# A four-layer graph network on one core: factors of a dense column moved between engines, and layer 2's block ends put in another order

## The chip, the cores and the metric

The kernel runs on one NeuronCore of a Trainium2 chip. The core has a matrix engine (TensorE, PE in the profile, with its weight loads shown apart as PEld), a vector engine (VectorE, DVE), a scalar engine (ScalarE, ACT), a general engine (GpSimd, POOL) and a queue engine (SyncE, SP). Each works through its own instructions in the order in which the program lists them, and waits at an instruction until what it needs is there; what stands behind it waits too. Sixteen DMA engines move data between the chip's main memory (HBM) and the on-chip memory (SBUF). Matmul results arrive in PSUM[...].

The metric is device microseconds (us) of one execution. The median of the runs shown decides.

## The reference

Four layers work on one graph of 3327 nodes with 512 features each. Every layer's result is added to its input and normalised over the features: `x = layernorm(x + layer(x, adj))`.

- Layer 0: graph attention, 8 heads of 64. Layer 1: mean over all neighbours, two dense maps. Layer 2: mean over the first 64 neighbours, two dense maps with a leaky ReLU.
- Layer 3: graph attention with 4 heads of 128, whose weight is built from quaternion parts. This is the layer that the change touches most:

```python
h = jnp.einsum('nf,hfo->hno', x, hamilton)
f_src = jnp.einsum('hno,ho->hn', h, a_src)
f_dst = jnp.einsum('hno,ho->hn', h, a_dst)
e = jax.nn.leaky_relu(f_src[:, :, None] + f_dst[:, None, :], ALPHA)
e = jnp.where((adj > 0)[None, :, :], e, NEG_INF)
attn = jax.nn.softmax(e, axis=-1)
h_prime = jnp.einsum('hnm,hmo->hno', attn, h)
```

with ALPHA = 0.2. The graph is uneven: an edge is the likelier the lower the two node numbers. So the first 128 nodes have many neighbours, and most nodes have some of those first 128 among theirs.

## The kernel before

**Blocks.** The nodes are cut into 26 blocks of 128 rows (NB = 26; the last has 127). Block 0 is nearly dense in both directions and is treated apart: its row (block 0 as the receiver, `row0`) and its column (block 0 as the source for every other block, `col0`) are dense 128 x 128 masks. All other edges are kept as lists. For block b a list has up to `NEAR[b]` places (1920 for block 1, down to 512 for the last three), in chunks of 128: 15 chunks for block 1, 4 for blocks 23 to 25.

**A group** is up to four chunks of one block. For each chunk GpSimd issues an indirect DMA that gathers 128 table rows from HBM (L1018, `gather`) into a ring of buffers. In layer 3 a group then passes these steps (`Gat.group`): distances `far` and the 0/1 matrix `ds` (ScalarE L1308, VectorE L1318), scores of the receivers by small matmuls (L1332), `sc` and its maximum (VectorE L1345, L1347), exponentials (ScalarE L1348, L1349), the selection matrix `sel` (L1353), the gathered rows times their weights (VectorE L1356), and matmuls into the block's sums in PSUM (L1375). Between the steps the generator yields.

**The order of the work** is written out by generators. `work` holds those of the groups, `ends` those of the block ends; `both()` lets every live generator of `work` take one step and then every one of `ends` (oldest first; in layer 3 newest first). One call of `both()` is a program step. In layer 2 and 3 the program order of each engine is just the order in which these steps issue instructions, and the tile framework adds the waits.

**Layer 2's ends and layer 3's projection** (`layer2_end`). When a block's neighbour sums are complete (matmuls L1879, with L1871 for block 0's column), its end divides (L2071), adds, takes the norm (L2073 to L851), and writes the new row block into `xres[b]`. Then it becomes the input of layer 3: `transposed` turns it by four TensorE transposes (L789) into PSUM and ScalarE copies the four parts to `xt` (L796), adding up row sums; `products` multiplies with the weights `w3` into two PSUM halves of two heads each (L1056, 16 matmuls, tile `po`, two buffers); `write` copies each half to the table rows `tg` (L1067, one buffer) and the scores `fall` (L1068), and stores the rows to HBM. `first_block` takes, from the same halves, the exponentials `ul` (L1241) and a copy of the features `G` (L1242), then a mask (L1244); on VectorE it makes the weights of this block as a source for block 0 (L1249, L1251). The matmuls with them, L1263, are issued by `catch_up`, one block at a time while groups are running; later blocks are put aside and done in `finish`.

Three things hold a block back in `layer2_end`: block 0 must have been opened (`opened`: `open_first` finds the bound `nmost` that all `ul` use), a space for G must be free (two spares of its own, and room in the ring once the last gather has been listed), and `g3.free` must be set. The block that passes clears `free`; `first_block` sets it after the mask.

After the last block's `write`, `head` finds the maxima over all nodes and stores three special table rows, on which layer 3's first gather waits. `finish` then computes, among others, `sh`, turns it by TensorE and stores it to the HBM scratch `e_d` (L1128), rows in the order head, block.

**Block 0's column in layer 3.** For every block b, `column` loads the exponentials of its 128 receivers for the four heads, the same to all 128 partitions (L1407, tile `upc`, three buffers), waits four steps, and makes the factors: four ScalarE instructions, `relu(rcol * up - 1)`, one per head because the scale is a value per partition and head (L1412); one step later one VectorE instruction adds 1 and applies the mask `col0` (L1414). The block's last group issues eight matmuls with them (L1372) ahead of its last chunk's. `open_column` prepares the other side once: it loads block 0's table rows to `gcol` (L1388), and from their scores makes `rcol` and the weights by which the rows are scaled (L1395 to L1400).

**Layer 3's ends** (`layer3_end`, `summed`): divide (L1522, L1523, L1526), ELU and residual (L1536, L1538, L1540), norm (L1541, L1542, L1552, L1553, L1556 to L1558), scale (L855), store.

Of the kernel before, what the change touches and what calls it, by code (L numbers as in the profile page):

```python
# [8 lines left out]
F32 = mybir.dt.float32  # L9
# [9 lines left out]
ALU = mybir.AluOpType  # L19
# [612 lines left out]
def sparse_path(ctx, tc, flag_i, x, adj, l0_w, l0_a1, l0_a2, l1_w_self, l1_b_self, l1_w_nb, l1_b_nb,  # L632
# [406 lines left out]
    class Gat:  # L1039
        def __init__(self, name, table, H, OUT, w, k):  # L1040
# [5 lines left out]
            self.opened, self.free = False, True  # L1046
# [12 lines left out]
        def write(self, b, pool, pw):  # L1059
# [5 lines left out]
            for s in range(2):  # L1065
# [3 lines left out]
                               by_head[:, :, 0:OUT + 2:OUT + 1].rearrange("p h k -> p k h"))  # L1069
            store(self.table, b, tb.rearrange("p h m -> p (h m)"), 2)  # L1070
# [37 lines left out]
        def finish(self, pool, ps):  # L1108
# [9 lines left out]
            if self.k:  # L1118
# [9 lines left out]
                nc.sync.dma_start(e_d, es)  # L1128
# [104 lines left out]
        def first_block(self, b, pool, pw, G, wt):  # L1233

            H, OUT = self.H, self.OUT
            hh = H // 2
            m = LAST if b == NB - 1 else P
            ul = pool.tile([P, H, 2], F32, name="ul")
            for s in range(2):
                by_head = pw[s].rearrange("p (h m) -> p h m", h=hh)  # L1240
                nc.scalar.activation(ul[:, s * hh:(s + 1) * hh, :], by_head[:, :, OUT + 1:], AF.Exp, bias=self.nmost)  # L1241
                nc.scalar.copy(G[:, s * hh:(s + 1) * hh, :OUT], by_head[:, :, 1:OUT + 1])  # L1242
            mask = pool.tile([P, P], F32, name="mk", bufs=1)
# [137 lines left out]
        def open_column(self, pool):  # L1381
# [6 lines left out]
            nc.sync.dma_start(gcol, self.table[2:2 + P, :])  # L1388
            self.gcol = gcol.rearrange("p (h m) -> p h m", m=M)
            self.rcol = pool.tile([P, H], F32, name="rcol", bufs=1)  # L1390
            self.low = pool.tile([P, 1], F32, name="low", bufs=1)
            nc.vector.memset(self.low, -1.0)
# [3 lines left out]
            nc.scalar.activation(self.rcol, low, AF.Exp, scale=1.0 - GAT_ALPHA)  # L1396
            nc.scalar.activation(self.gcol[:, :, OUT], low, AF.Exp, scale=GAT_ALPHA)
# [5 lines left out]
        def column(self, b, pool):  # L1403
# [3 lines left out]
            nc.sync.dma_start(up, bass.AP(tensor=e_d.tensor, offset=e_d.offset + b * P,  # L1407
                                          ap=[[0, P], [NB * P, H], [1, P]]))
            for _ in range(4):
                yield  # L1410
            for h in range(H):
                nc.scalar.activation(up[:, h, :], up[:, h, :], AF.Relu, bias=self.low, scale=self.rcol[:, h:h + 1])  # L1412
            yield
            nc.vector.scalar_tensor_tensor(up, up, 1.0, col0[:, b, None, :].to_broadcast([P, H, P]),  # L1414
                                           ALU.add, ALU.mult)
# [611 lines left out]
    with ExitStack() as lay:  # L2027
# [38 lines left out]
        def layer2_end(b, acc):  # L2066
# [12 lines left out]
            while b and not (g3.opened and (g3.spare or g3.space) and g3.free):  # L2079
                yield  # L2080
# [135 lines left out]
```

## Time and profile before

| what | value |
|---|---|
| median of 3 runs | 1661.63 us (1660.79 to 1669.61) |
| the profiled execution | 1659.49 us |
| its span, first to last instruction | 1657.7 us |
| TensorE matmuls busy | 1487.2 us (90%) |
| VectorE busy | 1175.7 us (71%) |
| ScalarE busy | 903.4 us (54%) |
| GpSimd busy | 762.6 us (46%) |
| TensorE weight loads busy | 998.9 us (60%) |
| mean granted TensorE clock | 0.955 |
| layer 3's projections (L1056) | 1158.2 to 1391.6 us of the span |
| layer 3's gathers | 1397.65 to 1614.04 us of the span |

A line of the profile names the source line, the engine, the operation, and what it writes and reads by the program's tile names, with shapes as partitions x elements. In a timeline the first number is the start in us from the beginning of the span and the second the time taken; `x4` says that four such instructions were merged into one line, `[1.41 <-ACT xt L796]` that the engine sat idle for 1.41 us until that instruction released it. In a view of stretches each engine's busy time is followed by its number of instructions. A view of waits gives the total in us, how often, and the longest. Instructions of one engine overlap at their edges, so a sum of durations is above the time that they occupy.

### The profile page before, as it was taken

Reading aid. Unit: us, or ns where it says so; the run is one execution under the profiler, and the core shown is the slowest. Engines: PE = TensorE matmul, PEld = TensorE weight load, DVE = VectorE, ACT = ScalarE, POOL = GpSimd, SP = SyncE. Lnnn points to the kernel's source line nnn. Section 1 sums busy time; section 2 is a strip of 40 time slices with the busy share of each in tenths; the row PEclk is TensorE's granted clock in tenths of the full one; section 3 lists DMA queues with packets and bytes.
Section 4 is the critical chain, followed back from the end, with each engine's and each line's share of the span. In section 5 each row is a group of like instructions: output and inputs, shape, how many; then the busy total and the mean of one; then the engine's idle time right before and its main releaser. Section 6 shows DMA issues by size and latency. Waiting matters only on the chain.

```text
span 1657.7 us, 24457 instructions
## 1 busy us (share of the span) xinstructions
PE 1487.2 (90%) x7305; PEld 998.9 (60%) x7341; DVE 1175.7 (71%) x3136; ACT 903.4 (54%) x3007; POOL 762.6 (46%) x994
## 2 busy tenths in 40 slices
PE   6789968999999999889999999887999996988885
PEld 4567746666666777435555555433566665777764
DVE  7998789998567789215566677648665644779886
ACT  5788865777667878412222121212344444679997
POOL 3000057665554520055444565137777702777770
PEclk9889979999999999879999999999999999999998
DMA  8877678876665542199788999348899812888881
GB/s 253 267 240 263 194 254 280 269 214 207 204 192 152 169 140 81 52 367 317 246 298 312 326 371 337 132 143 296 297 322 295 285 52 91 241 240 249 255 248 64
DMA packets 130402, 381.99 MB, mean 230 GB/s; under 512 B 22037, under 2 KB 36477, under 8 KB 130259
## 3 DMA queue, kind: packets, MB, share of 16 engines
q0 software_dynamic: 67696, 252.97, 47.6%
q1 hardware_dynamic: 62563, 127.35, 22.8%
q8 instruction: 60, 0.98, 0.2%
q14 instruction: 83, 0.68, 0.1%
HBM read 331.89 MB, written 48.37 MB: 229 GB/s over the span
## 4 chain that ended last, share of the span: by engine, by line
PE 63%; DVE 11%; ACT 9%; DMA 8%; issue 5%; POOL 3%; SPq 0%; ACTq 0%; DVEq 0%; POOLq 0%
PE po L806 19%; PE acc L1375 12%; PE po L1056 10%; PE acc L1879 9%; PE pt L789 3%; DMA gl<-t_d,idx 3%; DMA gt<-t_d,idx 1%; PE acc L1871 1%; PE acc L1263 1%; DVE gt L1356 1%; PE acct L1485 1%; DVE cand L909 1%; ACT m L882 1%; ACT upc L1412 1%; POOL gl L1018 1%
## 5 line engine op out<-in xcount | busy, mean ns | idle before, releaser
L1018 POOL DMA_INDIRECT gt<-t_d,idx x201 | 203.8, 1014 | 342.3 <-DVE eq L978 208.0
L1018 POOL DMA_INDIRECT gl<-t_d,idx x265 | 269.6, 1017 | 134.8 <-DMA t_d<-t 51.4
L1375 PE MATMUL acc<-gt,sel 128*128 128x264 f32 (+3 forms) x804 | 209.9, 408 | 4.4 <-DVE gt L1356 2.7
L1018 POOL DMA_INDIRECT gm<-t_d,idx x140 | 140.4, 1003 | 143.9 <-PE acc L1879 95.6
L806 PE MATMUL po<-wn,xt 128*128 128x512 f32 x416 | 193.9, 608 | 7.1 <-ACT h L1526 3.8
L1375 PEld LDWEIGHTS acc<-gt,sel 128*128 128x128 f32 (+3 forms) x804 | 153.4, 200 | 42.0 <-issue 13.9
L1375 PE MATMUL acc<-gl,sel 128*128 128x260 f32 (+3 forms) x524 | 137.5, 410 | 11.0 <-ACT r L1553 4.9
L806 PEld LDWEIGHTS po<-wn,xt 128*128 128x128 f32 x416 | 77.8, 194 | 89.1 <-issue 76.2
L1056 PE MATMUL po<-gt,xt 128*128 128x268 f32 x416 | 118.1, 428 | 14.1 <-ACT g0fall L1068 8.2
L1356 DVE TENSOR_TENSOR gt<-gt,pg 128x1536 f32<-128x1536 f32 (+3 forms) x64 | 116.6, 1822 | 13.6 <-ACT sel L1351 13.3
L792 ACT COPY xt<-pt 128x512 f32<-128x512 f32 x81 | 47.3, 588 | 130.8 <-PE pt L789 117.6
L1879 PE MATMUL acc<-gm,selr 128*128 128x512 f32 (+3 forms) x324 | 110.9, 462 | 7.3 <-DMA gm<-t_d,idx 5.0
L1375 PEld LDWEIGHTS acc<-gl,sel 128*128 128x128 f32 (+3 forms) x524 | 100.4, 201 | 27.1 <-ACT r L1553 5.2
L909 DVE MAX8 cand<-val 128x8 f32<-128x464 uint16 (+32 forms) x184 | 107.6, 620 | 0.1
L1056 PE MATMUL po<-w,xt 128*128 128x262 f32 x416 | 97.0, 386 | 8.0 <-ACT xt L796 5.1
L1018 POOL DMA_INDIRECT gk<-t_d,idx x65 | 65.7, 1011 | 82.3 <-DMA t_d<-mean 60.0
L1056 PEld LDWEIGHTS po<-gt,xt 128*128 128x128 f32 x416 | 79.2, 203 | 32.8 <-ACT g0fall L1068 8.6
L1308 ACT ACTIVATE far<-place,sites 128x128 int16<-128x128 int16 (+3 forms) x167 | 87.3, 543 | 13.1 <-DVE ds L1318 12.1
L806 PE MATMUL po<-wx,xt 128*128 128x512 f32 x208 | 93.6, 595 | 0.3 <-ACT vc L967 0.3
L789 PE MATMUL pt<-s_ident,xres 128*128 128x128 f32 x500 | 77.5, 283 | 17.7 <-POOL gt L1668 10.5
L806 PE MATMUL po<-wl,xt 128*128 128x512 f32 x208 | 93.1, 593 | 0.0
L1056 PEld LDWEIGHTS po<-w,xt 128*128 128x128 f32 x416 | 78.2, 190 | 24.0 <-ACT xt L796 9.8
(397 smaller groups left out, 3222.4 us busy)
## 6 DMA issues: line engine op xcount, KB each, us to landing
ab<-in_adj_dram SPq DMA_DIRECT2D x25, 832.0 KB
ab<-in_adj_dram SPq DMA_DIRECT2D x25, 831.5 KB
t_d<-t SPq DMA_DIRECT2D x25, 512.0 KB
gm<-t_d POOLq DMA_DIRECT2D x21, 512.0 KB
t_d<-t SPq DMA_DIRECT2D x25, 384.0 KB
t_d<-tg SPq DMA_DIRECT2D x25, 264.0 KB
gd<-t_d SPq DMA_DIRECT2D x25, 264.0 KB
t_d<-tg SPq DMA_DIRECT2D x25, 260.0 KB
```

The costliest lines, as they stand in the source:

```text
L789: nc.tensor.transpose(pt[:, c, :], src[:, c * P:(c + 1) * P], ident)
L792: nc.scalar.copy(xt, pt)
L806: nc.tensor.matmul(po, xt[:, c, :], w[:, c], start=c == 0, stop=c == DC - 1)
L882: nc.scalar.activation(m[:, c0:], ab[s][:, c0:], AF.Sign, accum_out=half[:, s, b:b + 1])
L909: nc.vector.max(out=cand[:, s, :], in_=val[:, cuts[s]:cuts[s + 1]])
L1018: nc.gpsimd.indirect_dma_start(out=t[:m, c, :], out_offset=None, in_=table[:, :], in_offset=bass.IndirectOffsetOnAxis(ap=l.idx[:m, c0 + c: ...
L1056: nc.tensor.matmul(pw[s], xt[:, c, :], self.w[:, c, s, :], start=c == 0, stop=c == DC - 1)
L1263: nc.tensor.matmul(self.acc[h // hh][:, h % hh, :], wt[:m, h, :], G[:m, h, :], start=False, stop=False)
L1308: nc.scalar.activation(o, place[:, (c0 + q0) * P:(c0 + q1) * P], AF.Abs, bias=l.nmid[k], scale=2.0)
L1356: nc.vector.tensor_mul(Gc[:, :, :OUT], Gc[:, :, :OUT], w[:, :g].rearrange("p c (h o) -> p (c h) o", o=1).to_broadcast([P, g * H, OUT]))
L1375: nc.tensor.matmul(accs[b][s], S[:m, c, :], G[:m, c, s * hh * M:(s + 1) * hh * M], start=at + c == 0, stop=last)
L1879: nc.tensor.matmul(accs[b], chosen, parts[:, k * D:(k + 1) * D], start=at + c + k == 0, stop=k == top and at + c == n - 1)
```

## The change

In layer 3, `column` makes the factors by VectorE alone: four instructions per block, one per head, each of which takes the larger of the loaded value and a value per partition (`least`) and multiplies with the mask. To make that the same product, `open_column` scales block 0's rows with the exponential of the full difference and keeps the reciprocal ratio in `least`. The factors are made in the step in which ScalarE's part was before, so the block's entry in `factors` is there one step earlier. `e_d` is stored in the order block, head, so that a block's load is one contiguous run. In `open_column` the load of `gcol` is issued where it was, and everything that uses it comes two steps later; a memset is gone.

In layer 2's ends, a block is turned (transposes and copy to `xt`) before it waits for the gate, not after it. A counter, `holding`, lets one block be turned and waiting until block 0 is open, and two after that. What needs the halves for block 0's sums, `ul` and `G`, is made in `lift`, which `write` calls after each half; for block 0 itself, whose bound is not there yet, it is called after `open_first`.

```diff
-            self.opened, self.free = False, True
+            self.opened, self.free, self.holding = False, True, 0
...
-        def write(self, b, pool, pw):
+        def write(self, b, pool, pw, lift=None):
...
+                if lift is not None:
+                    lift(s)
             store(self.table, b, tb.rearrange("p h m -> p (h m)"), 2)
...
-                nc.sync.dma_start(e_d, es)
+                nc.sync.dma_start(bass.AP(tensor=e_d.tensor, offset=e_d.offset,
+                                          ap=[[P, H], [H * P, NB], [1, P]]), es)
...
-        def first_block(self, b, pool, pw, G, wt):
-
-            H, OUT = self.H, self.OUT
-            hh = H // 2
-            m = LAST if b == NB - 1 else P
-            ul = pool.tile([P, H, 2], F32, name="ul")
-            for s in range(2):
+        def lifted(self, ul, G, pw):
+
+            OUT, hh = self.OUT, self.H // 2
+
+            def lift(s):
                 by_head = pw[s].rearrange("p (h m) -> p h m", h=hh)
                 nc.scalar.activation(ul[:, s * hh:(s + 1) * hh, :], by_head[:, :, OUT + 1:], AF.Exp, bias=self.nmost)
                 nc.scalar.copy(G[:, s * hh:(s + 1) * hh, :OUT], by_head[:, :, 1:OUT + 1])
+
+            return lift
+
+        def first_block(self, b, pool, ul, G, wt):
+
+            H = self.H
+            m = LAST if b == NB - 1 else P
...
             nc.sync.dma_start(gcol, self.table[2:2 + P, :])
+            for _ in range(2):
+                yield
             self.gcol = gcol.rearrange("p (h m) -> p h m", m=M)
-            self.rcol = pool.tile([P, H], F32, name="rcol", bufs=1)
-            self.low = pool.tile([P, 1], F32, name="low", bufs=1)
-            nc.vector.memset(self.low, -1.0)
+            self.least = pool.tile([P, H], F32, name="least", bufs=1)
             yield
             low = pool.tile([P, H], F32, name="lowf", bufs=1)
             nc.vector.tensor_sub(low, self.gcol[:, :, OUT], self.cmax)
-            nc.scalar.activation(self.rcol, low, AF.Exp, scale=1.0 - GAT_ALPHA)
-            nc.scalar.activation(self.gcol[:, :, OUT], low, AF.Exp, scale=GAT_ALPHA)
+            nc.scalar.activation(self.least, low, AF.Exp, scale=GAT_ALPHA - 1.0)
+            nc.scalar.activation(self.gcol[:, :, OUT], low, AF.Exp)
...
-            nc.sync.dma_start(up, bass.AP(tensor=e_d.tensor, offset=e_d.offset + b * P,
-                                          ap=[[0, P], [NB * P, H], [1, P]]))
+            nc.sync.dma_start(up.rearrange("p h i -> p (h i)"),
+                              bass.AP(tensor=e_d.tensor, offset=e_d.offset + b * H * P, ap=[[0, P], [1, H * P]]))
             for _ in range(4):
                 yield
             for h in range(H):
-                nc.scalar.activation(up[:, h, :], up[:, h, :], AF.Relu, bias=self.low, scale=self.rcol[:, h:h + 1])
-            yield
-            nc.vector.scalar_tensor_tensor(up, up, 1.0, col0[:, b, None, :].to_broadcast([P, H, P]),
-                                           ALU.add, ALU.mult)
+                nc.vector.scalar_tensor_tensor(up[:, h, :], up[:, h, :], self.least[:, h:h + 1], col0[:, b, :],
+                                               ALU.max, ALU.mult)
...
+            while b and g3.holding > g3.opened:
+                yield
+            g3.holding += 1
+            xt = transposed(fin, ps, xres[b], g3.xsum, b)
+            yield
             while b and not (g3.opened and (g3.spare or g3.space) and g3.free):
                 yield
+            g3.holding -= 1
             g3.free = False
             G, wt = g3.spaces()
-            xt = transposed(fin, ps, xres[b], g3.xsum, b)
-            yield
             pw = g3.products(ps, xt)
             yield
-            g3.write(b, fin, pw)
+            ul = fin.tile([P, H3, 2], F32, name="ul")
+            lift = g3.lifted(ul, G, pw)
+            g3.write(b, fin, pw, lift if b else None)
             if b == 0:
                 yield from g3.open_first(fin, ps, pacc0)
+                for s in range(2):
+                    lift(s)
             if b == NB - 1:
                 g3.head(fin, ps)
-            yield from g3.first_block(b, fin, pw, G, wt)
+            yield from g3.first_block(b, fin, ul, G, wt)
```

## The prediction

> **What bounds the kernel now.** I read the busy time of each engine in stretches first, because the page's 90% for TensorE averages over four layers. The cuts are where layer 2's projections begin (1180.4), where its last neighbour matmul ends (1368.4), where its last projection ends (1391.6), and two places in layer 3.
>
> ```profile
> core 0: us, PE busy (x) PEld busy (x) DVE busy (x) ACT busy (x) POOL busy (x), PEclk, DMA share, GB/s
> 1180.40:1368.40 188.00, 185.13 (x945) 128.74 (x963) 110.08 (x280) 83.12 (x419) 108.74 (x110) 1.00 0.73 246
> 1368.40:1391.60 23.20, 17.06 (x80) 13.66 (x79) 10.00 (x28) 11.48 (x64) 0.00 (x0) 1.00 0.10 39
> ...
> 1542.80:1628.60 85.80, 74.20 (x477) 59.58 (x474) 76.31 (x224) 81.77 (x258) 54.96 (x54) 0.92 0.79 230
> 1628.60:1657.70 29.10, 12.32 (x59) 10.08 (x57) 13.61 (x47) 18.32 (x49) 0.00 (x0) 0.74 0.14 49
> ```
>
> Layer 2 is TensorE's: idle 2.9 of 188 us, then 6.1 of 23.2. Layer 3's second half is ScalarE's (81.8 of 85.8 us), with VectorE close (76.3). Next the timeline, TensorE alone, at layer 2's end:
>
> ```profile
> 1369.43 3.80 PE L1056 MATMUL po<-w,xt 128*128 128x262 f32 x16 [0.46 <-ACT xt L796]
> 1373.07 0.60 PE L789 MATMUL pt<-s_ident,xres 128*128 128x128 f32 x4
> 1375.08 3.80 PE L1056 MATMUL po<-w,xt 128*128 128x262 f32 x16 [1.41 <-ACT xt L796]
> ...
> 1387.82 3.77 PE L1056 MATMUL po<-w,xt 128*128 128x262 f32 x16 [2.85 <-DVE xt L800]
> ```
>
> A projection each 5.65 us, 3.64 of it matmuls; the rest waits for xt, which ScalarE copies only after it has emptied the block before. Four projections come after the last neighbour matmul.
>
> Then layer 3's gathers and scores. These lines of GpSimd's and VectorE's timelines belong together:
>
> ```profile
> 1613.09 0.95 POOL L1018 DMA_INDIRECT gk<-t_d,idx  x1 [0.30 <-issue]
> ...
> 1628.59 0.20 DVE L1345 TENSOR_TENSOR sc<-pg,gk 128x32 f32<-128x32 f32 x1
> ```
>
> The last gather is issued by 1614.04; the score that needs it comes 14.6 us later. Going through all 57 groups so, the lag is 3 to 5 us up to 1543 (where the score itself waits 0.79 us for a gather) and then grows. GpSimd issues one gather each 1.25 us (0.95 busy, 0.30 between) from 1397.65 on, 165 of them, and is never held long. So up to about 1543 the gathers set the pace; after it the engines that work on them do, and fall some 10 us behind. Last, who VectorE and ScalarE wait for, from 1542.8 to 1628.6 and in the groups of layer 3:
>
> ```profile
> DVE upc L1414 <- ACT upc L1412: 3.4, 9, 0.6
> DVE h L1538 <- ACT e L1536: 2.9, 7, 0.6
> ...
> L1412 ACT ACTIVATE upc<-upc,low,rcol 128x128 f32<-128x128 f32 x100 | 40.8, 478 | 0.0
> L1414 DVE SCALAR_TENSOR_TENSOR upc<-upc,col 128x512 f32<-128x512 f32 x25 | 17.3, 691 | 6.2 <-ACT upc L1412 6.0
> ```
>
> **What the Trainium skill says.** "Perfetto Trace Analysis", section Identifying the Most-Contended Engine: for Vector and Scalar, occupancy names the bottleneck; the stretch above agrees with it (95% ScalarE). Section Optimizing Scalar/DVE Operations there: each instruction carries an overhead, so that larger ones pay if the engine is saturated; the change cuts one instruction into four. "VectorE: DVE Perf Modes", the section on the TRN2 errata: a fixed latency per instruction, paid per tile. The trace agrees: SCALAR_TENSOR_TENSOR takes 160 ns on 128x1 and 691 on 128x512. "ScalarE: Activation LUTs", Rules for kernel authors: relu, max and mul belong on VectorE; here 478 ns on ScalarE against 342 for a two-operation TENSOR_SCALAR of that shape (L1249).
>
> **Part 1, the factors.** Removed from ScalarE: four L1412 per block, 1.63 us end to end; 25 blocks, 40.8 us. On VectorE one L1414 goes, after which the next instruction starts 0.61 us later (1631.69 to 1632.30), and four SCALAR_TENSOR_TENSOR of 128x128 come. No row has them. From below: 160 ns at one element and 691 at 512 make about 293 at 128; less the 0.08 by which L1414 overlaps its successor, 0.21 each, 0.84 for four. From above: L1249's four take 1.11 us, 0.258 apart, so 1.03. I take 0.95: plus 0.34 per block. In 1542.8 to 1628.6 lie 11 blocks: VectorE 76.3 + 3.7 = 80.0. Its idle time there was 9.5 us: 3.4 for L1412 (gone), 2.9 for L1536 (ScalarE late; it loses 11 x 1.63 = 18 us of 81.8, so I let it go), 0.8 for a gather, 2.4 in small gaps, which stay. 80.0 + 2.4 = 82.4 against 85.8: **3.4 us gained**. VectorE is then the bound; what is late next is its own queue. Before 1543 the factors cost nothing, hidden by the gathers; without that cover, 14 x 0.34 = 4.8 us more.
>
> In the last stretch the chain of waits runs over L1412 twice (0.87 us at 1626.49, 1.63 at 1637.38), and TensorE's last factor matmuls (L1372) start 0.90 us late for it. The factors now come one step earlier in VectorE's order, before the last group's scaling is due. 0.87 + 1.63 + about 0.5 of the waits: **3.0 us gained**. From the last normalisation (1650.00) to the end nothing changes.
>
> **Part 2, column rows later.** The load of gcol is issued where it was; the instructions on it come two steps later. VectorE waited 1.02 us (L1395) and ScalarE 1.27 (L1396), with the first groups' ds, exp and sel queued behind. Worth nothing: by 1424.34 the scores wait for gathers anyway. Without that cover 2.3 us. The memset L1392 (0.06) goes too.
>
> **Part 3, order of e_d.** One store of 104 rows of 512 bytes as before; each of the 25 loads becomes 128 packets of 2 KB instead of 512 of 512 bytes. In the packet records these take 89 and 30 ns, so a load falls from 0.95 to 0.71 us of all 16 DMA engines, 6 us over 257. It is issued four steps ahead on SP, so nothing is gained directly; gathers may land a little sooner, hidden by the lag. Were they the bound, 1 or 2 us.
>
> **Part 4, layer 2's ends.** No instruction goes or comes; the order does. Before, one block held the gate from its transposes to its write: two program steps per block, a spare G held four. After, from its products to its write: one step, a G held three, so two blocks in three steps. The groups finish a block in about 2.2 steps (NEAR, at most four chunks per group). The blocks that queued up before the first one opened are thus worked off in some 25 steps, and I count two projections after the last neighbour matmul instead of four.
>
> As TensorE is full, work moved forward delays the last neighbour matmul: 2 x (3.64 + 0.44 transposes) = 8.2 us. The catch-up matmuls (L1263, 0.90 us a block) of three blocks, which stood in finish (48 of them at 1394.39 and 1397.99; 24 stay), move forward too: 2.7 us. Of the 2.9 us idle I let 2.0 go. The last neighbour matmul ends at 1368.3 + 8.2 + 2.7 - 2.0 = 1377.2. Then two dependency chains stand bare. The last block but one ended its neighbours 3.3 us before: from there 5.2 us to its transposes (as 1362.82 to 1368.16), 1.06 to its products, 3.64 for them, so 6.6 us after 1377.2. The last block's e (L2071) queues on ScalarE behind that block's xt, 7.0 us after the same start; 5.0 to its transposes, 2.4 for these, xt and the row sum xs, 3.7 for products: 18.1 - 3.3 = 14.8. Layer 2's projections end at 1392.0 against 1391.6: **0.4 us lost**. From below: half of the 6.1 us idle gained, 3 us. From above: back-to-back projections, nine pairs by my count. Between two of them ScalarE must do transposes' wait 0.6, xt 1.0 and half a write 0.9, 2.5 us, while TensorE has 0.44 + about 2.0 + 0.90 = 3.3 of cover; an e (0.7) and Ln/Exp (0.5) in between make 3.7 and 0.4 of stall a pair, 4 us. The halves in turn free the first PSUM half two ScalarE instructions sooner (half of the 0.9), inside that sum. The single buffer of tg now sees writes one step apart: store issue to landing was about 2 us unloaded and 4.4 loaded, under a step of about 5. SP has nothing else there, and GpSimd's gathers have slack: they were done at 1326.
>
> **Sum.** -3.4 - 3.0 + 0.4 = -6.0 us. The profiled execution took 1659.5 us, 1.8 outside its span of 1657.7; it becomes 1653.5. The median of the runs shown, 1661.6, lies 2.1 above it; the same difference gives 1655.6.
>
> **Rivals.** (a) The small instructions cost more: with VectorE the bound, layer 3's bulk gains nothing once four take 1.25 us (0.31 each, where 9.5 - 2.4 - 11 x (1.25 - 0.61) is zero). For it: fp8 input, a pointer scalar. Against: L1249 has two pointers and starts each 0.258. 1661.6 - 3.0 + 0.4 = 1659. (b) The whole 10 us lag goes, since with ScalarE at 75% nothing stalls VectorE: 10 + 3 - 0.4, 1649; against it, VectorE's own 80 us. (c) Layer 2 gains after all, its idle time falling from 9 to 4 and the moved L1263 covered: -6.4 - 4, 1651. (d) Slower: ScalarE's in-order queue takes the gate's place in layer 2. Its Ln waited for VectorE up to 2.4 us; if each back-to-back pair stalls that long, 9 x 2.4 = 21.6 us against 6.4 gained, 1677; it decides from 0.7 us a pair. For it: ScalarE already waits for TensorE at every xt; against: a whole step lies between e and Ln. (e) The moved yields leave the factors as late as before, the tail gains only its 1.63: 1657.
>
> **How the numbers follow.** Forecast, -2 to -9: 0.45. (a) and (e): 0.13. (b): 0.20. (c): 0.13. (d): 0.09. The bound of 0.5% (8.3 us) is about what a measurement of this kernel can tell from no change. Faster by more: (b), (c) and a fifth of the forecast, 0.42. Slower by more: 0.07 of (d). The rest 0.51. The range runs from 1647, (b) with something of (c), to 1663; the forecast's own is 1652 to 1660.
>
> **What would show it.** Right: no L1412 on ScalarE; four instructions 0.21 to 0.26 us apart per block; VectorE over 93% and ScalarE under 80% in the stretch before the last score; that score 10 to 12 us after its gather instead of 14.6; two projections after layer 2's last neighbour matmul; the first layer 3 gather within 3 us of 1397.65. Wrong: waits of TensorE for the PSUM halves or xt all through layer 2, or four factors over 1.25 us.

## The result

The changed kernel takes 1656.5 us (median of 12 runs, 1651.5 to 1658.9) where the kernel before takes 1661.9 beside it: a ratio of 0.9956, interval 0.9943 to 0.9969. The two medians lie 5.5 us apart; the ratio puts the gain at some 7 us (5 to 9). The forecast was 1655.6, 6.0 us of gain. The total came out close; one of its three terms came to nothing and another was too small, and the experiments below are mostly about these two.

The profiled execution of the changed kernel has a span of 1652.4 us (1657.7 before). Cut at the same events, the two compare so:

| stretch, us | before | after |
|---|---|---|
| start of the span to layer 2's first projection | 1158.2 | 1155.4 |
| first projection to last neighbour matmul | 210.1 | 218.4 |
| last neighbour matmul to last projection | 23.3 | 16.2 |
| last projection to first gather of layer 3 | 6.1 | 6.3 |
| first gather to last score | 230.9 | 232.1 |
| last score to start of last o | 21.4 | 16.2 |
| last o to the end | 7.8 | 7.9 |

The first line is code that the change leaves alone; over the ten kernels profiled up to `end_early` below it lies between 1155 and 1161, so that its 2.8 us are within the scatter. Layer 3 as a whole, first gather to end, fell from 260.1 to 256.2.

First the busy times of the changed kernel in stretches, cut where those of before were cut (columns: window, its length, then busy time and instructions of PE, PEld, DVE, ACT, POOL, the granted TensorE clock, DMA share, GB/s). The first line begins, here as in the prediction, where the first block behind block 0 is turned (1177.05, and 1180.4 before); layer 2's first projection, that of block 0, stands some 22 us ahead of it.

```profile
1177.05:1373.80 196.75, 194.99 (x1005) 137.18 (x1021) 112.84 (x287) 85.70 (x444) 105.19 (x108) 1.00 0.72 239
1373.80:1389.97 16.17, 10.57 (x41) 7.87 (x40) 6.45 (x19) 6.28 (x34) 0.00 (x0) 0.89 0.04 17
1389.97:1542.80 152.83, 127.10 (x857) 107.25 (x857) 125.46 (x362) 93.31 (x281) 111.96 (x188) 0.92 0.79 234
1542.80:1628.30 85.50, 73.45 (x494) 60.58 (x493) 80.47 (x257) 67.23 (x216) 51.16 (x53) 0.96 0.74 226
1628.30:1652.40 24.10, 8.02 (x44) 6.56 (x42) 12.98 (x49) 14.41 (x39) 0.00 (x0) 0.77 0.18 60
```

TensorE is idle 1.8 of 196.8 us in layer 2, so no new wait stands there. In layer 3's second half VectorE is now busy 94% (80.5 of 85.5 us) and ScalarE 79%: the bound has changed engines as forecast. But the stretch has become no shorter. All of layer 3's gain lies in the last line, 24.1 us instead of 29.1.

TensorE's timeline at layer 2's end, changed kernel:

```profile
1376.48 3.80 PE L1056 MATMUL po<-w,xt 128*128 128x262 f32 x16 [0.46 <-ACT xt L796]
1381.95 0.66 PE L789 MATMUL pt<-s_ident,xres 128*128 128x128 f32 x4 [1.67 <-DVE xres L851]
1384.51 5.46 PE L1056 MATMUL po<-w,xt 128*128 128x262 f32 x16 [1.90 <-DVE xt L800]
```

Two projections follow the last neighbour matmul (it ends at 1373.80), not four. The second took 5.46 us for matmuls that take 3.8 elsewhere: the granted clock over them was 0.69.

GpSimd's last gather of the changed kernel, then VectorE's last score:

```profile
1608.87 0.95 POOL L1018 DMA_INDIRECT gk<-t_d,idx  x1 [0.30 <-issue]
```

```profile
1628.31 0.20 DVE L1353 TENSOR_TENSOR sc<-pg,gk 128x32 f32<-128x32 f32 x1
```

The score stands 18.5 us behind its gather, not 10 to 12, and not even the 14.6 of before: counted from the first gather, the last gather comes 2.8 us sooner than before (212.6 us, 215.4 before) and the last score 1.1 us later. One of VectorE's groups over layer 3, and its one wait from 1542.8 to 1628.3 (total in us, times, longest), say that the new instruction waits for nobody, but that one of the two old waits is still there:

```profile
L1420 DVE SCALAR_TENSOR_TENSOR upc<-upc,least,col 128x128 f32<-128x128 f32 x100 | 28.3, 344 | 0.0
```

```profile
DVE h L1544 <- ACT e L1542: 1.7, 4, 0.5
```

Four runs (`late_but_last3_means`, `full_change_again`, `rows_early`, `late_last3_means_2`) were made while every kernel, the one before included, took some 100 us longer, 44 of them in layer 3 in the full change's profile, where gathers came more slowly; their ratios stand against the kernel before in that condition and are not compared with the others.

### The profile page after: what moved, and what is told of

The parts are those of the page before. It is cut to its first block, busy times and chain, and to the rows that moved or that the text cites. A ratio compares the mean times of both kernels' runs of the same rounds, so it can differ in the third digit from the quotient of the medians.

```text
span 1652.4 us, 24419 instructions
## 1 busy us (share of the span) xinstructions
PE 1483.7 (90%) x7306; PEld 998.8 (60%) x7341; DVE 1182.3 (72%) x3210; ACT 866.2 (52%) x2907; POOL 753.2 (46%) x992
## 4 chain that ended last, share of the span: by engine, by line
PE 59%; DVE 13%; ACT 8%; DMA 8%; issue 5%; POOL 3%; SPq 0%; POOLq 0%; DVEq 0%; ACTq 0%
PE po L806 20%; PE acc L1885 10%; PE acc L1383 9%; PE po L1056 9%; PE pt L789 3%; DMA gl<-t_d,idx 3%; DMA gt<-t_d,idx 2%; PE acc L1271 1%; PE acc L1877 1%; DVE gl L1364 1%; PE acct L1491 1%; ACT h L1532 1%; POOL gl L1018 1%; DVE upc L1420 1%; DVE e L1546 1%
## 5 line engine op out<-in xcount | busy, mean ns | idle before, releaser
L1018 POOL DMA_INDIRECT gl<-t_d,idx x265 | 263.3, 994 | 156.8 <-DMA t_d<-t 52.6
L1383 PE MATMUL acc<-gl,sel 128*128 128x260 f32 (+3 forms) x524 | 133.4, 400 | 18.2 <-issue 9.3
L1056 PE MATMUL po<-gt,xt 128*128 128x268 f32 x416 | 114.0, 417 | 14.3 <-ACT g0fall L1068 9.0
L796 ACT ACTIVATE xt<-pt 128x128 f32<-128x128 f32 (+1 forms) x208 | 55.6, 287 | 90.6 <-PE pt L789 90.4
```

The costliest lines, as they stand in the source:

```text
L796: nc.scalar.activation(xt[:, c, :n], pt[:, c, :n], AF.Identity, accum_out=xsum[:, c, b:b + 1])
L1018: nc.gpsimd.indirect_dma_start(out=t[:m, c, :], out_offset=None, in_=table[:, :], in_offset=bass.IndirectOffsetOnAxis(ap=l.idx[:m, c0 + c: ...
L1056: nc.tensor.matmul(pw[s], xt[:, c, :], self.w[:, c, s, :], start=c == 0, stop=c == DC - 1)
L1383: nc.tensor.matmul(accs[b][s], S[:m, c, :], G[:m, c, s * hh * M:(s + 1) * hh * M], start=at + c == 0, stop=last)
```

## The experiments

All profiled kernels side by side. The scores are counted from 1 to 57; "bulk" is the 28th to the last score, the part in which scores no longer wait for gathers; "tail" the last score to the last o; "layer 3" the first gather to the end. The ratio is against the kernel before in the same group of runs; its median was 1661.9 us beside the full change, 1662.2 beside the next four kernels and 1663.1 beside the last four.

| kernel | time, us | ratio (interval) | bulk | tail | layer 3 |
|---|---|---|---|---|---|
| before | 1661.9 | 1 | 110.7 | 21.4 | 260.1 |
| full change | 1656.5 | 0.9956 (0.9943 to 0.9969) | 111.6 | 16.2 | 256.2 |
| columns_only | 1656.8 | 0.9971 (0.9959 to 0.9984) | 111.9 | 16.3 | 257.1 |
| ends_only | 1661.2 | 0.9990 (0.9976 to 1.0004) | 110.4 | 21.4 | 260.8 |
| factors_late | 1654.1 | 0.9953 (0.9937 to 0.9969) | 107.3 | 19.2 | 253.8 |
| rows_512 | 1656.3 | 0.9968 (0.9955 to 0.9982) | 112.0 | 16.2 | 256.5 |
| before_early | 1659.1 | 0.9973 (0.9962 to 0.9984) | 111.5 | 16.6 | 258.8 |
| late_but_last3 | 1653.5 | 0.9935 (0.9915 to 0.9956) | 108.3 | 16.2 | 252.3 |
| late_means_by_act | 1653.8 | 0.9931 (0.9908 to 0.9955) | 102.9 | 19.8 | 250.1 |
| end_early | 1658.2 | 0.9971 (0.9960 to 0.9981) | 111.1 | 16.2 | 257.2 |

**Which half of the change gains: layer 3 alone, layer 2's ends alone.** The first kernel is the one before with the functions open_column and column and the order of e_d changed, and nothing else:

```
-                nc.scalar.activation(up[:, h, :], up[:, h, :], AF.Relu, bias=self.low, scale=self.rcol[:, h:h + 1])
-            yield
-            nc.vector.scalar_tensor_tensor(up, up, 1.0, col0[:, b, None, :]..., ALU.add, ALU.mult)
+                nc.vector.scalar_tensor_tensor(up[:, h, :], up[:, h, :], self.least[:, h:h + 1], col0[:, b, :],
+                                               ALU.max, ALU.mult)
```

> The kernel before with the three layer 3 parts alone (factors by VectorE, column rows later, order of e_d); layer 2's ends as before. Theory (the whole gain is layer 3's): 6 to 8 us under the kernel before, ratio about 0.996, within 1.5 us of the full change; the stretch from the last score to the last o about 16 us as in the full change (21.4 before); the first layer 3 gather 295 us after the start of layer 2, as before. Rival (layer 2's ends carry a part): only 3 to 5 us under before, and 3 us or more above the full change.

The second is the one before with the rest of the change:

```
+            while b and g3.holding > g3.opened:
+                yield
+            g3.holding += 1
+            xt = transposed(fin, ps, xres[b], g3.xsum, b)
+            yield
             while b and not (g3.opened and (g3.spare or g3.space) and g3.free):
                 yield
+            g3.holding -= 1
...
-            xt = transposed(fin, ps, xres[b], g3.xsum, b)
```

> The kernel before with layer 2's ends alone (turn ahead of the gate, halves copied in turn, one program step of gate instead of two); layer 3 as before. Theory (work moved, none saved): within 1.5 us of the kernel before; two projections after the last neighbour matmul instead of four, that matmul 8 to 9 us later against the opening of layer 2; opening to the last projection 212 to 216 us as before. Rival (layer 2 gains): 3 to 4 us under before, the idle time of TensorE in layer 2 down from 9 to 5 us.

Layer 3 alone gives 4.8 us (2.7 to 6.8), the ends alone 1.7 (a gain of 4.0 to a loss of 0.7); together 6.5, against 7.3 for both in one. Stretches of layer 3 in the two profiles, from the 34th score to the last and from there to the end; first `columns_only`, then `ends_only`:

```profile
1548.02:1633.85 85.83, 73.66 (x494) 60.72 (x493) 80.53 (x257) 67.33 (x216) 50.54 (x52) 0.96 0.72 222
1633.85:1658.60 24.75, 8.00 (x44) 6.54 (x42) 12.96 (x49) 14.39 (x39) 0.00 (x0) 0.77 0.17 58
```

```profile
1545.50:1631.77 86.27, 75.06 (x480) 59.67 (x479) 76.53 (x224) 82.62 (x259) 54.76 (x55) 0.92 0.77 230
1631.77:1661.02 29.25, 12.18 (x60) 10.23 (x59) 13.60 (x47) 18.32 (x49) 0.00 (x0) 0.73 0.13 48
```

The first is the full change over again (VectorE 94%, 24.8 us at the end), the second the kernel before (ScalarE 96%, 29.3). So layer 3's gain needs nothing of layer 2's ends. The time of `columns_only` alone doesn't decide: 4.8 us is less than the theory's 6 to 8 and within the rival's 3 to 5, though the kernel isn't 3 us above the full change, as the rival wanted (1656.8 against 1656.5). In layer 2, first to last projection takes 233.4, 234.1 and 233.4 us in the three kernels with the old ends (before, columns_only, before_early), and 234.5, 233.0, 234.8, 233.7, 236.3 and 234.6 in those with the new ones (full change, ends_only, factors_late, rows_512, late_but_last3, late_means_by_act): 0.9 us more in the mean, with a scatter as large. The profiles show no gain there; the interval of the time doesn't exclude one.

**The step earlier.** The change also takes a yield out, so that VectorE does the factors one program step sooner. Put back:

```
-            for _ in range(4):
+            for _ in range(5):
                 yield
             for h in range(H):
                 nc.vector.scalar_tensor_tensor(up[:, h, :], ...
```

> The full change, but the four factor instructions one program step later (five yields instead of four), where the old one stood in VectorE's order. Theory A (the tail gains because the factors come ahead of the last group's scaling): TensorE's last factor matmuls wait for them again, last score to last o 1 to 2.5 us longer than the 16.2 us of the full change, time 1 to 2.5 us more. Theory B (the tail gains by ScalarE's relief alone): within 0.5 us of the full change. In the bulk both expect no difference: VectorE does the same work.

Both theories missed: the tail did get 3.1 us longer (19.2), but the bulk, where no difference was expected, got 4.4 us shorter (107.3 instead of 111.6), and layer 3 as a whole 2.4 shorter. The stretch from the 34th score to the last, `factors_late`:

```profile
1545.58:1628.38 82.80, 72.89 (x484) 58.85 (x484) 79.72 (x258) 68.60 (x215) 53.96 (x55) 0.98 0.79 239
```

82.8 us, of which VectorE is busy 79.7. The reason stands in the timelines of the same pair of groups. VectorE in the full change:

```profile
1602.49 0.18 DVE L1529 RECIPROCAL rden<-rden 128x4 f32<-128x4 f32 x1
...
1603.22 1.75 DVE L1364 TENSOR_TENSOR gl<-gl,pg 128x1536 f32<-128x1536 f32 x1
...
1605.79 0.69 DVE L1544 SCALAR_TENSOR_TENSOR h<-h,xres 128x512 f32<-128x512 f32 x1 [0.34 <-ACT e L1542]
...
1607.32 1.14 DVE L1420 SCALAR_TENSOR_TENSOR upc<-upc,least,col 128x128 f32<-128x128 f32 x4
```

and with late factors:

```profile
1602.90 0.18 DVE L1529 RECIPROCAL rden<-rden 128x4 f32<-128x4 f32 x1
...
1603.62 1.17 DVE L1420 SCALAR_TENSOR_TENSOR upc<-upc,least,col 128x128 f32<-128x128 f32 x4
1604.72 1.74 DVE L1364 TENSOR_TENSOR gl<-gl,pg 128x1536 f32<-128x1536 f32 x1
...
1606.86 0.68 DVE L1544 SCALAR_TENSOR_TENSOR h<-h,xres 128x512 f32<-128x512 f32 x1
```

Between rden (L1529) and the h that needs its answer (L1544) ScalarE must do the four h and the e, behind what already stands in its queue. ScalarE in the full change:

```profile
1602.93 0.61 ACT L1302 COPY gl<-zeros 32x8 f32<-32x8 f32 x3
1603.55 0.51 ACT L1316 ACTIVATE far<-place,sites 128x256 int16<-128x256 int16 x1
1603.97 1.12 ACT L1532 ACTIVATE h<-acc,rden 128x128 f32<-128x128 f32 x4
1605.13 0.63 ACT L1542 ACTIVATE e<-h 128x512 f32<-128x512 f32 x1
```

And in the kernel before, where rden is done at 1602.99, two lines of ScalarE and the h of VectorE that waits for them:

```profile
1602.29 1.63 ACT L1412 ACTIVATE upc<-upc,low,rcol 128x128 f32<-128x128 f32 x4
...
1606.74 0.63 ACT L1536 ACTIVATE e<-h 128x512 f32<-128x512 f32 x1
...
1607.40 0.69 DVE L1538 SCALAR_TENSOR_TENSOR h<-h,xres 128x512 f32<-128x512 f32 x1 [0.61 <-ACT e L1536]
```

Two stretches thus begin at rden. ScalarE's, up to the end of e, takes 3.08 us in the full change. ScalarE is idle for only 0.08 of it: 1.25 goes to other work that stands in front (the rest of a `sel`, three copies of zeros, `far`), 1.75 to h and e. VectorE's own work up to h takes 2.64, and VectorE waits for what is missing. In the kernel before the two were 4.38, with 0.9 us of the old factor instructions in it and two small exponentials behind them, and 3.33, with L1414 in it. So the change shortens ScalarE's stretch by 1.3 us, but its order takes 0.7 out of VectorE's as well, and a wait stays. Late factors leave ScalarE's stretch as it is (3.04) and put the four factor instructions into VectorE's (3.65): h finds e ready. In all 14 blocks of the bulk ScalarE is idle for less than 0.1 us of its stretch, in both kernels.

In the full change VectorE stands still ahead of h in 9 of these 14 blocks, for 0.13 to 0.55 us. In the bulk these waits sum to 2.7 of the 4.4 us in the full change and to nothing with late factors. Another 1.05 is no loss: early, one set of factors more lies ahead of the last score (60 instructions instead of 56), which the tail then does without. The remaining 0.6 is busy time of other instructions, too spread out to be named; all other gaps sum to 3.9 us in both. The other three kernels with the change's order and engine have bulks of 111.1 to 112.0 us, so that the difference isn't that of one execution; the times, known to some 2 us either way, don't settle it (7.8 us of gain with late factors, 7.3 for the full change).

**The same order with the old engine.** To part order from engine, the kernel before with both of its factor steps one program step earlier:

```
-            for _ in range(4):
+            for _ in range(3):
                 yield
             for h in range(H):
                 nc.scalar.activation(up[:, h, :], up[:, h, :], AF.Relu, bias=self.low, ...
```

> The kernel before, its factors still shared by ScalarE and VectorE, but both one program step earlier (three yields instead of four): the order of the change without its engine. With the kernel before, the full change and the one with late factors it makes two by two: engine against order. Theory (order and engine act apart): from the last score to the last o about 2 to 3 us less than the 21.4 of before, since the order alone was worth 3.1 us of the tail with VectorE's factors; from the first gather to the last score 2 to 4 us more than the 230.9 of before, because one set more lies ahead of the last score (0.6) and VectorE has less between rden and the step that waits for ScalarE's e; in all within 1.5 us of before. Rival (the order costs only where VectorE carries all four factors): first gather to last score within 1 us of before, and the whole 2 us faster.

First gather to last score 234.4 us, tail 16.6. Of the 3.5 us that the first got longer, 2.6 lie ahead of the 28th score, where gathers set the pace, and 0.9 in the bulk, 0.6 of them the set that moved. In the bulk VectorE's wait for ScalarE's factors grew from 3.4 to 5.4 us, while its wait for e fell from 2.9 to 1.9, where the theory had it grow: the old factor instructions no longer stand between rden and e on ScalarE. First gather to last o, two by two:

| | order of before | one step earlier |
|---|---|---|
| ScalarE and VectorE | 252.4 (before) | 251.0 (before_early) |
| VectorE alone | 246.3 (factors_late) | 248.3 (full change) |

The engine is worth 6.1 us in the old order; the step earlier gains 1.4 with the old engine and costs 2.0 with the new one. The first theory's sum holds (within 1.5 us), though the tail gained 4.8 where it had 2 to 3. The rival falls: it wanted the first gather to the last score unchanged. These are single profiled executions, and one line of the table can be some tenths off: columns_only and rows_512 repeat the full change's 248.3 with 248.7 and 248.4. By its time before_early gains 4.5 us (2.7 to 6.3), three more than this table gives it and more than the theory's 1.5.

**The order of e_d.** The full change with 512-byte rows again:

```
-                nc.sync.dma_start(bass.AP(tensor=e_d.tensor, offset=e_d.offset,
-                                          ap=[[P, H], [H * P, NB], [1, P]]), es)
+                nc.sync.dma_start(e_d, es)
...
-            nc.sync.dma_start(up.rearrange("p h i -> p (h i)"),
-                              bass.AP(tensor=e_d.tensor, offset=e_d.offset + b * H * P, ap=[[0, P], [1, H * P]]))
+            nc.sync.dma_start(up, bass.AP(tensor=e_d.tensor, offset=e_d.offset + b * P,
+                                          ap=[[0, P], [NB * P, H], [1, P]]))
```

> The full change, but e_d in its old order: each of the 25 loads reads rows of 512 bytes again (512 packets instead of 128). Theory (hidden): within 1 us of the full change; the gathers of layer 3 may take up to 2 us longer from first to last, which the lag between gather and score covers. Rival (DMA descriptors set the pace of the first half of layer 3): 2 to 4 us slower than the full change, the stream of gathers back at 215 us from 212.6.

First to last gather 212.8 us (212.6 with 2 KB packets), layer 3 256.5 (256.2). The 384 of 512 packets that the change saves on each of these loads were worth nothing that shows; the rival falls.

**Late, but early at the end.** The step earlier costs through a wait that only the bulk has, and helps the tail. So, on the full change:

```
-            for _ in range(4):
+            for _ in range(5 if b < NB - 3 else 4):
```

> The full change with the factors one program step later for all blocks but the last three. Theory (the step earlier costs the bulk through VectorE's wait for e, and helps only at the very end, where TensorE waits for the last factors): 27 scores from the one at 120 us to the last take 107 to 109 us as with late factors (111.6 in the full change), last score to last o 16 to 17 us (19.2 with late factors, 16.2 in the full change); together 3 to 4 us less than the full change, 10 to 11 under the kernel before. Rival (what late factors save in the bulk comes back at the end whatever the order): as with all factors late, 2 us less than the full change.

```profile
1546.10:1629.88 83.78, 75.76 (x491) 61.17 (x491) 80.70 (x261) 68.56 (x215) 54.11 (x54) 0.96 0.79 235
1629.88:1653.58 23.70, 8.41 (x46) 6.89 (x44) 12.96 (x49) 14.38 (x39) 0.00 (x0) 0.78 0.17 60
```

These are its stretches from the 34th score to the last and to the end: the short bulk (83.8 us, with the one set more, and no wait for e) and the short tail together. Layer 3 takes 252.3 us, 3.9 less than the full change, and the time is 10.8 us under the kernel before (7 to 14), as the theory said. The intervals of the times overlap with those of late factors and of the full change, so it is the profile that sets the versions apart.

**Is VectorE really the bound?** If it is, taking any instruction off it shortens the bulk by that instruction. On the kernel with late factors, the two 128x1 instructions per block that scale the mean go to ScalarE (in short; the run's code does so by a parameter, in layer 3 alone):

```
-        nc.vector.tensor_mul(nm[:, 0:1], nm[:, 0:1], rs)
+        nc.scalar.mul(nm[:, 0:1], nm[:, 0:1], rs)
...
-            nc.vector.tensor_scalar(nm[:, 0:1], nm[:, 0:1], -1.0 / D, None, ALU.mult)
+            nc.scalar.mul(nm[:, 0:1], nm[:, 0:1], -1.0 / D)
```

> Late factors for all blocks, and the two instructions per block of 128x1 that scale the mean (150 and 160 ns on VectorE) on ScalarE. Theory (with late factors VectorE is the bound of the second half without a gap): 14 blocks times 0.15 to 0.3 us, 2 to 4 us less from the score at 120 us to the last than the 107.3 of late factors. Rival (ScalarE is as near: its chain from rden to e grows by 0.4 us per block, and VectorE's wait for e comes back): within 1 us of late factors, with VectorE idle before h again.

```profile
1544.80:1624.00 79.20, 72.84 (x484) 59.18 (x484) 76.62 (x235) 71.89 (x236) 53.49 (x55) 0.96 0.82 252
```

The bulk fell by 4.3 us (2 to 4 were expected), from 107.3 to 102.9: 14 blocks times 0.31 us, the whole duration of the two instructions. ScalarE took 21 of them in this stretch (199 and 278 ns each) without making VectorE wait. So VectorE bounded that stretch to the last tenth, and still does (76.6 of 79.2 us). The tail lost 0.5 us, since there the small instructions stand on ScalarE's own chain. The time is 11.5 us under the kernel before (7 to 15).

Both edits together were run twice, each time while gathers came late:

> Both edits together: late factors for all blocks but the last three, and the two small instructions on the mean by ScalarE. Theory (the two act on different things, the first on VectorE's wait for e and the last wait of TensorE, the second on the length of VectorE's queue): 57th score 222 to 225 us after the first gather, last score to last o 16 to 17 us, layer 3 in all 247 to 249 us (256.2 in the full change, 252.3 and 250.1 with one edit alone); 7 to 9 us under the full change, 14 to 16 under the kernel before. Rival (at the end the small instructions on ScalarE take back what the early last factors save): 250 us for layer 3, as with the means alone.

> Both edits together once more, where gathers land as fast as in the first runs of this study. Theory (the two edits add up): the last score 222 to 225 us after the first gather, last score to last o 16 to 17 us, layer 3 in all 247 to 249 us (256.2 in the full change); 7 to 9 us under the full change, ratio to the kernel before 0.990 to 0.992. Rival (they don't add up): 250 us for layer 3, ratio 0.993 to 0.994 as with the means alone.

Ratios 1.0009 (0.9991 to 1.0027) and 1.0008 (0.9992 to 1.0024), layer 3 298.8 us both times. The full change beside the first of them:

> The full change itself, beside the version above. Every theory: 6 to 8 us under the kernel before; 232 us from the first gather to the last score, 16.2 from there to the last o.

1763.2 us, ratio 1.0028 (1.0006 to 1.0050): there the change is some 5 us slower than the kernel before (1 to 9). Its profile, first gather to 28th score and from there to the last:

```profile
1462.56:1622.00 159.44, 114.63 (x698) 91.13 (x698) 97.22 (x270) 72.57 (x216) 105.63 (x182) 0.81 0.69 204
1622.00:1737.78 115.78, 97.44 (x633) 79.71 (x634) 105.07 (x329) 86.39 (x273) 57.96 (x59) 0.96 0.65 192
```

VectorE does the same 97 and 105 us of work as in the first profile of this kernel, but its first half takes 159 us instead of 120. The gathers come 1.52 us apart instead of 1.30 (248.7 and 212.6 us from the first to the 165th), and the longest wait ahead of a score is 14.9 us; why they come late no run shows. An engine that waits for data isn't made faster by less work. The tail was unmoved: 16.2 us for the full change and 17.0 for both edits. Whether the two edits add up where gathers are fast remains open; so does why the full change is behind the kernel before there (6 to 8 us of gain were expected), since no profile of it was taken in that condition.

**The column rows.** The full change without the two empty steps:

```
             nc.sync.dma_start(gcol, self.table[2:2 + P, :])
-            for _ in range(2):
-                yield
```

> The full change without the two empty steps ahead of the first instruction on the column rows: it waits again where it did. Theory (hidden, since by 27 us after the first gather the scores wait for gathers anyway): first gather to the 13th score 54 to 56 us as in every kernel, time within 1 us of the full change. Rival (the start of layer 3 is not covered): 1 to 2.5 us slower, the lag carried through to the last score.

It has the same late gathers. First gather to 13th score 75.0 us, against 75.1 of the full change beside it; layer 3 299.3 against 299.8; ratio to the kernel before 1.0008 (0.9994 to 1.0021). No difference that shows, as the theory said, though late gathers cover more than early ones would.

**Layer 2's last two chains, an attempt that failed.** In the full change the last block's e (L2077) starts at 1377.07, behind the copies of xt of the block before, though its sum was complete at 1373.80. So the last block begins a step earlier and goes first in each step:

```
         def layer2_end(b, acc):
-            yield
+            if b < NB - 1:
+                yield
...
         g3.space = space
+        ends.newest = True
         while work.live or ends.live:
```

> The full change, but the end of layer 2's last block starts one program step earlier and ahead of the block before it in each step, so that its e isn't queued on ScalarE behind the copies of xt of that block. Theory (the 16.2 us from the last neighbour matmul to the last projection are two dependency chains one after the other, by ScalarE's order): the chains overlap, 12.5 to 14 us, all that follows 2.5 to 3.5 us earlier, and the time 2 to 3.5 us less than the full change. Rival (TensorE's own work and the transposes bound it): less than 1 us.

TensorE's timeline there:

```profile
1379.08 6.56 PE L1056 MATMUL po<-w,xt 128*128 128x262 f32 x16 [2.43 <-ACT xt L796]
1385.47 0.60 PE L789 MATMUL pt<-s_ident,xres 128*128 128x128 f32 x4
1388.06 5.49 PE L1056 MATMUL po<-w,xt 128*128 128x262 f32 x16 [1.99 <-ACT gl L1243]
```

The chains did not overlap; last neighbour matmul to last projection became 19.1 us instead of 16.2. The last block's Ln now stands on ScalarE ahead of the other block's xt and holds it back, so that TensorE's wait for this xt grows from 0.46 to 2.43 us; the last block's transposes then queue on TensorE behind the other's projection; and this projection took 6.56 us at a clock of 0.57. Both theories missed. It was one more in-order queue in which the earlier item made the later one wait.

## Why the prediction was right, and where it was wrong

**Layer 3's bulk (-3.4): wrong.** The step that failed stands in the text: "2.9 for L1536 (ScalarE late; it loses 11 x 1.63 = 18 us of 81.8, so I let it go)". And of "the factors now come one step earlier in VectorE's order" only the tail was costed. The price was about right: four instructions hold VectorE's queue for 1.05 us, forecast 0.95 (bounds 0.84 to 1.03, just missed). But what ScalarE loses over the whole stretch isn't what it loses between rden and e. At the pair shown above it lost 1.3 us of 4.4 there, and VectorE's own work meanwhile lost 0.7 of 3.3, because the new instructions no longer stand in that place. In the stretch of the forecast 2.0 of the 2.9 us therefore stayed (1.7 in the view above, which leaves out two waits of 0.13), and one set more came ahead of the last score (1.05). One reading was off too: the wait of 0.8 for a gather ends at 1542.83, where the stretch begins, and doesn't lie in it; so 3.1 us of small gaps had to stay, not 2.4, and the sum comes to 83.1. With late factors, the order of the kernel before, it comes out: 79.7 us of work and 3.1 of gaps make 82.8. In the order of the change it became 86.2, against 85.8 before: gain nothing. Rival (a) forecast just that, by a price of 1.25 which isn't so.

**Layer 3's tail (-3.0): gained, but too small, and mostly by the term that was counted least.** It gained 5.2. In the order of before, the engine is worth 2.2 (21.4 to 19.2), where 0.87 + 1.63 had been counted, and the earlier step then 3.1 (19.2 to 16.2), where "about 0.5 of the waits" stood. But the two overlap: the earlier step alone, with ScalarE still at work on the factors, gains 4.8 (`before_early`, 16.6), and the engine then 0.4. Of the 3.1, 1.05 is the set that the bulk now pays. The other 2.0 isn't a wait of TensorE for factors: in the tail with late factors its only wait over 0.15 us is one of 0.9, for rden. What the traces show is that the last block's rden starts 12.4 us after the last score with late factors and 9.6 in the full change; from there to the last o it is 6.9 and 6.6.

So two errors of opposite sign met: layer 3 was to gain 6.4 us and gained 3.9 by its profile. Rival (b), the whole lag gone, fell: the lag grew to 18.5 us. Rival (e) fell too: the factors come earlier, and the tail gains more than 1.63.

**Layer 2 (+0.4): right by the profile.** Two projections instead of four, as counted; first projection to last neighbour matmul 8.3 us longer, where the working has 8.9; then 16.2 to the last projection where it has 14.8, 1.7 of them the slow clock of the last projection. Old and new ends differ by 0.9 us in the mean of nine profiles. Rival (d), stalls between back-to-back projections, fell: TensorE idles 1.8 of 196.8 us. Rival (c), a gain of 4 us, isn't seen in any profile, but the time of ends_only alone (a gain of 4.0 to a loss of 0.7) doesn't rule it out.

**Column rows and e_d (0 each): right**, each by its own run, the first only under late gathers.

**What stays open.** The profiles place some 3 us of gain: 3.9 in layer 3, less 0.9 in layer 2. For layer 3 the time of `columns_only`, 4.8 us (2.7 to 6.8), agrees with this. For the whole, the medians say 5.5 and the ratio 7 (5 to 9). The rest can't be put down to a quick execution of the kernel before: both profiled executions were quick by about as much, 1659.5 against a median of 1661.9 and 1654.2 against 1656.5. Layer 2's ends may hold some of it (up to 4.0 by the time of `ends_only`); where, no profile shows. That the total came within 1 us of the forecast is therefore luck as far as the profiles go: they account for about half of it.

## What to carry to other kernels

An engine can be free a fifth of the time and still hold another one up at most blocks. What counts is the work that stands in its queue between the question and the answer, against the work that the asking engine has of its own meanwhile. Here both were shortened at once, and two thirds of the wait stayed; putting work back on the asker's side removed it. Moving ScalarE's other work (`sel`, the zeros, `far`) behind h and e might do the same from the other side; it was not tried. So before moving an instruction to an earlier step, ask whose answer it was covering. When the bound moves to another engine, look at once for small instructions on the new one: two of 150 and 160 ns per block were worth as much in the bulk as the whole placement of the factors.

## What the runs showed of the hardware

Four SCALAR_TENSOR_TENSOR of 128x128 with a per-partition scalar and an fp8 third operand take 1.05 us of VectorE's queue, 0.26 apart (343 ns for one alone); one instruction on 128x512 held it for 0.61. Almost as close stand two-operation TENSOR_SCALARs of that shape without a third operand (0.258), so the fp8 operand costs nothing that shows.

The sixteen matmuls of one projection took 3.8 us at full clock, 5.46 at a granted 0.69 and 6.56 at 0.57, all at layer 2's end. Kernels with the same order of work there got 3.77 (before) and 5.46 (columns_only, before_early) for the last projection, and the full change itself 5.46 and, in `full_change_again`, 3.77; so a difference of 1.7 us in that place says nothing of a change.
